# A state-space scan across five engines: tanh for the gate's Silu, and four instructions moved in the pipeline

## The chip, the cores and the metric

The kernel runs on one core of one Trainium2 chip. A core has TensorE (PE in the profile; its weight loads are shown as PEld), VectorE (DVE), ScalarE (ACT), GpSimd (POOL) and SyncE (SP, which here only issues DMAs). Each engine takes its instructions in the order of its own list; engines wait for one another through semaphores. The metric is the device time of one execution in microseconds (us).

## The reference

Two layers follow each other on an image batch of 4 x 48 x 48 x 128; each adds its result to its input. The change touches the first layer alone, a state-space scan over the image in four directions. Cut to what matters:

```python
xz = einsum(gn(x), in_proj_w); xin, z = split(xz)          # 256 channels each
xc = silu(depthwise_conv3x3(xin) + conv_b)
xs = [rows, columns, rows reversed, columns reversed] of xc  # K = 4 directions, L = 2304
dts_r, Bs, Cs = split(x_proj_w[k] @ xs[k])                   # 8, 16 and 16 rows
dt = softplus(dt_proj_w[k] @ dts_r + dt_proj_b)
for l in range(L):                                           # per channel, 16 states n
    h[n] = h[n] * exp(dt[l] * A[n]) + dt[l] * xs[l] * B[n, l]
    y[l] = sum(h[n] * C[n, l] for n in range(16))
y = sum of the four directions, turned back, + Ds * xs
out = out_proj_w @ (layernorm(y) * silu(z))
x = x + out
```

## The kernel before, in words

All work of the first layer is written out by hand in one order for every engine (`Ordered`, line 40, which is why the profile shows line 54 for nearly all of it). For each of 4 images the four directions run in the order k = 0, 2, 1, 3; each direction is cut into 5 chunks along the sequence, four of 480 places and one of 384. Within a chunk the 16 states are 16 steps. One step covers both halves of the 256 channels in one scan instruction of 2 x 480 + 2 places on VectorE.

Even and odd steps get their input dt * x * B in two ways:

- An even step: `spread` lets TensorE lay row B over all partitions in PSUM (`pb`, one bank); `drive_in` multiplies it with `du` on VectorE into `db`. Its decay exp(dt * A) is written by ScalarE into PSUM (`decay_here`, tile `da`, one buffer).
- An odd step: `scale` multiplies a transposed `du` (`turned`) with B as a per-partition factor on ScalarE (`scaled`, four instructions); `turn` transposes it back on TensorE into PSUM (a `da` bank, one buffer). Its decay is written by ScalarE to SBUF (`decay_there`, tiles `decay`, two buffers).

Then, for both, VectorE scans (`scan`, output `h`), GpSimd multiplies with row C (`read_out`, `hc`; the row `cbc` comes broadcast from DRAM by `fetch`, in ROWS = 5 buffers) and saves the carry; TensorE sums the `hc` of the states in PSUM by transposing into the same place (`sum_plain`, `sum_turned`, tiles `yp`, 16 instructions per pair of steps). After a chunk's last step `put_away` copies the sums to SBUF on ScalarE and lets a `gather` bring them back and add them to `y`.

`advance` (line 739) runs for each new step. It goes through the list `LAGS` (lines 733 to 736): a pair (3, fetch) means that `fetch` is issued for the step that came 3 steps ago. So the place in the list and the lag set the order in which each engine finds its instructions.

Everything else is cut into pieces by Python generators with `yield`: projecting the next direction's chunks (`project_chunk`: px, xd, pd, dt, bt), the next image's input projection and convolution (`front`: pj, pc, xc, pad), transposing `du` (`turn_du`: pdu), gathering (`gather`: pg, y or yb), and the end of an image's chunk (`back`: layer norm, gate, output projection; tile `ws`, matmuls pm, pv, pz, po, pr). `piece()` runs one piece, from one `yield` to the next; it is called at the end of each `advance`, and once more by `extra` for an odd step when more than one generator waits. Pieces use one PSUM bank in common (`side`, tag `pp`), so a piece's matmul waits until ScalarE or VectorE has read the one before.

The gate in `back` (lines 475 to 486): z = Silu(x W + b) from one instruction over both halves, after the norm's Ln and Exp; GpSimd multiplies it to `ys`. ScalarE holds one set of function tables at a time, and `ACT_TABLE_LOAD` changes it.

`done[0]` tells the projection of coming chunks which chunk has been used up, so that it may write to its `dt` and `bt` buffers again.

Of the kernel before, what the change touches and what calls it, by code (L numbers as in the profile page):

```python
# [12 lines left out]
AF = mybir.ActivationFunctionType  # L13
ALU = mybir.AluOpType
# [9 lines left out]
NF = D // 128  # L24
N = 16
# [6 lines left out]
LC = 480  # L32
GAP = 2
LB = 128
RING = 6
ROWS = 5
CHUNKS = [(s, min(LC, L - s)) for s in range(0, L, LC)]


# [18 lines left out]
def first_layer(ctx, tc, io, x1_dram, sp_dram, d_w, d_m):  # L58
# [9 lines left out]
    on = Ordered(tc)  # L68
# [9 lines left out]
    ps_y = ctx.enter_context(tc.tile_pool(name="l0_psy", bufs=1, space=PSUM))  # L78
    rows = ctx.enter_context(tc.tile_pool(name="l0_rows", bufs=ROWS))
    dram = ctx.enter_context(tc.tile_pool(name="l0_dram", bufs=8, space=DRAM))  # L80
# [60 lines left out]
    def side(name):  # L141
        pool, tag = banks[0]
        if not begun[0]:
            banks.rotate(-1)
        return pool.tile([128, 512], F32, tag=tag, name=name)
# [6 lines left out]
    def at(tile_, k, s, n):  # L152

        if k % 2 == 0:
            return tile_[:, :, s : s + n]
        return tile_.rearrange("p f (h w) -> p f w h", w=H)[:, :, s // T : (s + n) // T, :]

    def like(ap, k):

        return ap if k % 2 == 0 else ap.rearrange("p (w h) -> p w h", h=T)  # L160
# [6 lines left out]
    def open_up(b, x, made):  # L167

        xc = two.tile([128, NF, L], F32, tag="xc", name=f"xc{b}")
        made["xc"] = xc  # L170
        st = small.tile([128, 6, 6], F32, tag="st", name=f"st{b}", bufs=1)
        for q in range(6):
            on.vector.bn_stats(st[:, q], x[:, 0, q * 384 : (q + 1) * 384])
            if q % 2:
                yield FREE
        mv = small.tile([128, 2], F32, tag="mv", name=f"mv{b}")
        on.vector.bn_aggr(mv, st)
        aff = small.tile([128, 2], F32, tag="aff", name=f"aff{b}")
        group_affine(on, small, ps_s, gmat, eps, mv[:, 0:1], mv[:, 1:2], aff[:, 0:1], aff[:, 1:2], 1, f"g{b}")
        yield FREE  # L180
        wb = small.tile([128, 2 * NF], F32, tag="wb", name=f"wb{b}")
        pw = side(f"pw{b}")
        for q in range(2 * NF):
            on.tensor.matmul(
                pw[:, q : q + 1], w_in[:, q * 128 : (q + 1) * 128], aff[:, 1:2], start=True, stop=True
            )
        on.scalar.copy(wb, pw[:, 0 : 2 * NF])
        w = two.tile([128, 2 * D], F32, tag="w", name=f"w{b}")
        on.gpsimd.tensor_scalar(w, w_in, aff[:, 0:1], None, ALU.mult)
        made["w"], made["wb"] = w, wb  # L190
        yield FREE
# [163 lines left out]
    def blocks(n):  # L355

        return [(q, min(LB, n - q * LB)) for q in range(-(-n // LB))]
# [95 lines left out]
    def back(b, s, n, yb, x, w, wb):  # L453


        t = f"{b}_{s}"
        xs = at(x, 1, s, n)[:, 0]
        ys = yb[:, :, 0:n]
        ws = one.tile([128, (T + 2) * (H + 2)], F32, tag="pad", name=f"ws{t}")
        z = ws[:, 0 : NF * LC].rearrange("p (f n) -> p f n", f=NF)  # L460
        rs, xo = ws[:, NF * LC : (NF + 1) * LC], ws[:, (NF + 1) * LC : (NF + 2) * LC]
        pm = side(f"pm{t}")
        for f in range(NF):
            on.tensor.matmul(pm[:, 0:n], lnmat, yb[:, f, 0:n], start=(f == 0), stop=(f == NF - 1))
        yield
        on.vector.tensor_sub(ys, ys, pm[:, None, 0:n].to_broadcast([128, NF, n]))
        yield FREE
        on.scalar.activation(z[:, :, 0:n], ys, AF.Square)
        pv = side(f"pv{t}")
        for f in range(NF):  # L470
            on.tensor.matmul(pv[:, 0:n], lnmat, z[:, f, 0:n], start=(f == 0), stop=(f == NF - 1))
        yield

        on.scalar.activation(rs[:, 0:n], pv[:, 0:n], AF.Ln, bias=eps)
        for f in range(NF):
            pz = side(f"pz{t}_{f}")
            on.tensor.matmul(
                like(pz[:, 0:n], 1), w[:, D + f * 128 : D + (f + 1) * 128], xs, start=True, stop=True
            )
            yield  # L480
            if f == 0:
                on.scalar.activation(rs[:, 0:n], rs[:, 0:n], AF.Exp, scale=-0.5)
            on.scalar.activation(z[:, f, 0:n], pz[:, 0:n], AF.Identity, bias=wb[:, NF + f : NF + f + 1])
        on.scalar.activation(z[:, :, 0:n], z[:, :, 0:n], AF.Silu)
        yield FREE
        on.gpsimd.tensor_mul(ys, ys, z[:, :, 0:n])
        yield FREE
        po = side(f"po{t}")
        for f in range(NF):
            on.tensor.matmul(po[:, 0:n], w_out[:, 0, f], yb[:, f, 0:n], start=(f == 0), stop=(f == NF - 1))  # L490
        yield
        on.vector.tensor_mul(xo[:, 0:n], po[:, 0:n], rs[:, 0:n])
        pr = side(f"pr{t}")
        on.tensor.matmul(like(pr[:, 0:n], 1), ident, xs, start=True, stop=False)
        yield
        for f in range(NF):
            on.tensor.matmul(pr[:, 0:n], w_out[:, 1, f], z[:, f, 0:n], start=False, stop=(f == NF - 1))
        yield
        on.vector.tensor_add(xo[:, 0:n], xo[:, 0:n], pr[:, 0:n])
        last = b == B - 1 and s == 0  # L500
        (nc.scalar if last else nc.sync).dma_start(
            x1_dram[b].rearrange("w h t -> w (h t)")[:, s : s + n], xo[:, 0:n]
        )
        yield FREE
# [32 lines left out]
    def spread(u):  # L537

        c, i, n = u.c, u.i, u.c.n
        if i == N - 1:  # L540
            done[0] = c.number + 1
        if u.turned:
            return
        u.pb = ps_b.tile([128, 512], F32, tag="pb", name=f"pb{c.t}_{i}")
        for q, r in blocks(n):
            on.tensor.transpose(
                u.pb[:, q * LB : q * LB + r], c.bt[0:r, q, i : i + 1].to_broadcast([r, 128]), ident[0:r, 0:r]
            )
# [43 lines left out]
    def decay(u, turned):  # L592

        c, i, n = u.c, u.i, u.c.n
        if u.turned != turned:
            return
        da, o = (decays[i // 2 % 2], LC) if turned else (das[0], BANK - GAP)
        for f in range(NF):
            q = c.k * NF + f
            x = o + GAP if f else o - n  # L600
            on.scalar.activation(da[:, x : x + n], c.dt[:, f, 0:n], AF.Exp, scale=a_neg[:, q, i : i + 1])
        u.da = da[:, o - n : o + GAP + n]
# [48 lines left out]
    def gather(c, yt):  # L651
# [29 lines left out]
        if final:  # L681
            backs.append(back(c.b, s, n, yb, c.im["x"], c.im["w"], c.im["wb"]))
            later.append(backs[-1])
# [25 lines left out]
    done = [0]  # L709
# [17 lines left out]
    def drain(gen):  # L727
        while gen in later:
            piece()


    decay_here, decay_there = partial(decay, turned=False), partial(decay, turned=True)
    LAGS = (
        (3, fetch), (2, open_db), (4, drive_in), (5, scan), (4, decay_here), (3, spread), (4, turn), (3, decay_there),
        (2, extra), (2, scale), (5, read_out), (5, carry_on), (8, sum_plain), (7, sum_turned), (8, put_away),
    )
    window = deque([None] * 9, 9)

# [44 lines left out]
    for j, chunks in enumerate(directions):  # L783
# [9 lines left out]
        for m, c in enumerate(chunks):  # L793
            c.carry = carries[j % 2]
            for i in range(N):
# [7 lines left out]
                if m + 1 < len(chunks):  # L803
                    f = (6, 10).index(i) if i in (6, 10) else None
# [4 lines left out]
                elif nxt is not None:  # L809
                    f = (9, 12).index(i) if i in (9, 12) else None  # L810
# [19 lines left out]
def layer0(tc, io, x1_dram):  # L830

    io["first"] = partial(first_layer, tc, io, x1_dram)


def group_affine(nc, pool, psum, gmat, eps, mean, var, scale, shift, n, name):


    pm = psum.tile([128, 512], F32, tag="pp", name=f"gm_{name}")
    mc = pool.tile([128, n], F32, tag="gmc", name=f"gmc_{name}")
    nc.vector.tensor_copy(mc, mean)  # L840
    nc.tensor.matmul(pm[:, 0:n], gmat, mc, start=True, stop=True)
    gm = pool.tile([128, n], F32, tag="gm", name=f"gmean_{name}")
    nc.vector.tensor_copy(gm, pm[:, 0:n])
    d = pool.tile([128, n], F32, tag="gd", name=f"gd_{name}")
    nc.vector.tensor_sub(d, mc, gm)
    nc.vector.tensor_mul(d, d, d)
    nc.vector.tensor_add(d, d, var)
    pv = psum.tile([128, 512], F32, tag="pp", name=f"gv_{name}")
    nc.tensor.matmul(pv[:, 0:n], gmat, d, start=True, stop=True)
    sd = pool.tile([128, n], F32, tag="gs", name=f"gs_{name}")  # L850
    nc.scalar.activation(sd, pv[:, 0:n], AF.Sqrt, bias=eps)
    nc.vector.reciprocal(scale, sd)
    nc.vector.tensor_mul(shift, gm, scale)
    nc.vector.tensor_scalar_mul(shift, shift, -1.0)
# [1255 lines left out]
```

## Time and profile before

| | us |
|---|---|
| median of 3 runs (5062.57 to 5072.48) | 5067.83 |
| the profiled execution's own time | 5056.55 |
| its span | 5054.8 |
| PE busy | 4215.2 (83%) |
| DVE busy | 3822.8 (76%) |
| ACT busy | 3635.6 (72%) |
| POOL busy | 3367.5 (67%) |
| mean granted TensorE clock | 0.918 |

The first layer ends at about 4276 us of the span, where its last result is issued; the second layer takes the rest and is not changed. Busy times are sums over the whole span. "Idle before" is time that an engine spent without work just ahead of an instruction, and the name behind the arrow is what ended that wait. Starts in a timeline are in microseconds from the span's start.

### The profile page before, as it was taken

To read this page: it belongs to the slowest core of one execution; us is meant where nothing else is said; L and a number is where in the kernel's file an instruction comes from. 1 tells how busy PE (TensorE), PEld (TensorE's weight loads), DVE (VectorE), ACT (ScalarE), POOL (GpSimd) and SP (SyncE) were. 2 spreads that over 40 slices of the span, in tenths; PEclk is the share of its full clock that TensorE was granted. 3 is DMA by queue.
4 is the path that set the end of the run, shared out by engine and by line. 5 is a ranking of instruction groups with operands and counts; after the bars stand their busy time and mean duration, and the time that the engine had idled before them with its cause. 6 is when DMAs were issued, how large, how long until landed. Compare 5 with 4: busy or idle time off the path is not lost.

```text
span 5054.8 us, 73887 instructions
## 1 busy us (share of the span) xinstructions
PE 4215.2 (83%) x26332; PEld 3091.3 (61%) x26332; DVE 3822.8 (76%) x2574; ACT 3635.6 (72%) x7167; POOL 3367.5 (67%) x3533
## 2 busy tenths in 40 slices
PE   6888988887899888878998988787878786779976
PEld 3566766665666666656666666566666663445543
DVE  1587889877878898778788987788888985457636
ACT  3677788877777888787778887878888884413344
POOL 2476778766867787668676886677777874047631
PEclk8999999989999999899999998999999997889977
DMA  1122323222322232223232332223333323226546
GB/s 34 56 74 64 88 81 90 79 69 77 79 74 87 76 90 79 69 68 89 72 89 75 90 83 71 68 82 87 88 85 86 84 78 83 48 53 162 127 110 158
DMA packets 306204, 417.99 MB, mean 83 GB/s; under 512 B 110804, under 2 KB 285012, under 8 KB 305260
## 3 DMA queue, kind: packets, MB, share of 16 engines
q1 hardware_dynamic: 300256, 410.19, 30.5%
q8 instruction: 208, 3.41, 0.3%
q10 hardware_dynamic: 5580, 3.08, 0.2%
q14 instruction: 160, 1.31, 0.1%
HBM read 377.99 MB, written 35.38 MB: 82 GB/s over the span
## 4 chain that ended last, share of the span: by engine, by line
PE 47%; ACT 23%; DVE 12%; issue 7%; POOL 3%; DMA 2%; SPq 1%; DVEq 0%; ACTq 0%; POOLq 0%
PE yp L54 12%; DVE h L54 7%; PE da L54 6%; ACT scaled L54 5%; PE pg L54 5%; PE pc L54 4%; ACT da L54 4%; ACT decay L54 4%; PE pd L54 3%; PE px L54 3%; DVE db L54 3%; PE pb L54 2%; ACT dt L54 2%; ACT L54 2%; ACT ws L54 1%
## 5 line engine op out<-in xcount | busy, mean ns | idle before, releaser
L54 POOL TENSOR_TENSOR hc<-h,cbc 128x960 f32<-128x960 f32 (+1 forms) x1280 | 2540.2, 1985 | 1107.4 <-DVE h L54 665.1
L54 DVE TENSOR_TENSOR_SCAN h<-da,carry,db 128x962 f32<-128x962 f32 (+1 forms) x640 | 1359.6, 2124 | 369.5 <-ACT da L54 361.7
L54 DVE TENSOR_TENSOR_SCAN h<-decay,carry,da 128x962 f32<-128x962 f32 (+1 forms) x640 | 1365.5, 2134 | 25.5 <-PE da L54 18.5
L54 PEld LDWEIGHTS yp<-ident,hc 128*128 128x128 f32 (+1 forms) x9728 | 1180.3, 148 | 301.2 <-issue 166.4
L54 PE MATMUL yp<-ident,hc 128*128 128x128 f32 (+1 forms) x9728 | 1297.5, 289 | 63.9 <-ACT turned L54 28.7
L54 ACT ACTIVATE scaled<-turned,bt 128x256 f32<-128x256 f32 (+1 forms) x2432 | 1035.5, 497 | 3.7 <-PE da L54 3.7
L54 DVE TENSOR_TENSOR db<-du,pb 128x960 f32<-128x960 f32 (+1 forms) x640 | 704.8, 1101 | 408.5 <-PE pb L54 397.8
L54 ACT ACTIVATE da<-dt,a_neg 128x480 f32<-128x480 f32 (+1 forms) x1280 | 828.5, 647 | 175.3 <-DVE h L54 153.0
L54 ACT ACTIVATE decay<-dt,a_neg 128x480 f32<-128x480 f32 (+1 forms) x1280 | 791.4, 665 | 0.0
L54 PE MATMUL da<-ident,scaled 128*128 128x128 f32 (+1 forms) x4864 | 648.4, 277 | 107.5 <-DVE h L54 88.7
L54 PEld LDWEIGHTS da<-ident,scaled 128*128 128x128 f32 (+1 forms) x4864 | 553.4, 146 | 136.5 <-ACT decay L54 52.0
L54 PEld LDWEIGHTS pb<-ident,bt 128*128 128x128 f32 (+1 forms) x2432 | 295.1, 143 | 218.2 <-issue 173.4
L54 PE MATMUL pb<-ident,bt 128*128 128x128 f32 (+1 forms) x2432 | 381.9, 279 | 5.6 <-DVE db L54 5.4
L54 PE MATMUL pc<-pad,cdiag 128*128 128x480 f32 (+1 forms) x630 | 283.1, 574 | 8.8 <-ACT pad L54 8.8
L54 POOL TENSOR_TENSOR du<-dt,xc 128x480 f32<-128x480 f32 (+1 forms) x160 | 205.3, 1283 | 72.8 <-ACT dt L54 72.8
L1527 PE MATMUL acc<-v,attn_c 128*64 128x384 f32 x1152 | 207.6, 498 | 30.1 <-DVE v L1519 16.1
L1523 POOL TENSOR_TENSOR v<-grep,xrep 128x768 f32<-128x768 f32 x96 | 175.0, 1824 | 86.5 <-PE acc L1527 44.3
L54 ACT ACT_TABLE_LOAD x147 | 188.6, 1283 | 58.6 <-PE gv_l L54 35.1
L54 PE MATMUL px<-xc,w_xp 128*40 128x480 f32 (+1 forms) x320 | 214.0, 768 | 16.3 <-ACT xc L54 12.3
L1519 DVE TENSOR_TENSOR v<-gp,xrep 128x1536 f32<-128x1536 f32 x96 | 167.9, 1756 | 73.6 <-PE acc L1527 41.0
L54 PE MATMUL pdu<-ident,du 128*128 128x128 f32 (+1 forms) x608 | 110.9, 308 | 127.1 <-ACT turned L54 122.0
L54 PE MATMUL pg<-ident,turned 128*128 128x128 f32 x608 | 110.8, 303 | 124.4 <-ACT turned L54 93.2
(375 smaller groups left out, 4646.0 us busy)
## 6 DMA issues: line engine op xcount, KB each, us to landing
cbc<-cd SPq DMA_DIRECT2D x1024, 240.0 KB
cbc<-cd SPq DMA_DIRECT2D x256, 192.0 KB
xrep<-dxt SPq DMA_DIRECT2D x48, 576.0 KB
grep<-dgt SPq DMA_DIRECT2D x16, 576.0 KB
x<-in_xT SPq DMA_DIRECT2D x16, 288.0 KB
xr<-in_xT SPq DMA_DIRECT2D x16, 288.0 KB
da_m<-a_m SPq DMA_DIRECT2D x24, 192.0 KB
a_m<-da_m SPq DMA_DIRECT2D x32, 144.0 KB
```

What stands on the lines that cost most here:

```text
L54: return lambda *args, **kw: self._tc.keep_in_program_order(emit(*args, **kw))
L1519: nc.vector.tensor_mul(v, gp[:, None, :, 0:NC].to_broadcast([128, 2, 2, NC]), x[:, :, 0:2])
L1523: nc.gpsimd.tensor_mul(v3, r[:, 2:3].to_broadcast([128, 2, NC]), x[:, :, 2])
L1527: nc.tensor.matmul(acc[c][64 * b : 64 * b + 64, 0:NC], attn_c[:, 2 * pair + b, g, q], v[:, b, c] if c < 2 else v3[:, b], start=first, stop ...
```

## The change

Four things change together in the first layer.

1. The gate is computed as (tanh(a/2) + 1) * (a/2) with a = x W + b, which is Silu(a). The second half of the bias `wb` is stored halved; per half of the channels ScalarE writes a/2 into `z` and tanh(a/2) into a new view `th` of the same `ws` tile; then one VectorE instruction forms (th + 1) * z, ahead of GpSimd's multiplication.
2. `spread` moves from lag 3, ahead of `turn`, to lag 2 at the end of the list, behind the sums of the even step. One call of `piece()` lies between its old and its new place.
3. `decay_there` moves from lag 3 (behind `decay_here`) to lag 2, right behind `scale`; `extra` moves behind both. `put_away` moves from the end of the list to its beginning.
4. `fetch` moves from lag 3 to lag 1, and ROWS goes from 5 to 6.

`done[0]` is now set in `decay` for step N - 2, which is issued in the same `advance` as before.

```diff
-ROWS = 5
+ROWS = 6
...
-        on.scalar.copy(wb, pw[:, 0 : 2 * NF])
+        on.scalar.copy(wb[:, 0:NF], pw[:, 0:NF])
+        on.scalar.activation(wb[:, NF : 2 * NF], pw[:, NF : 2 * NF], AF.Copy, scale=0.5)
...
         z = ws[:, 0 : NF * LC].rearrange("p (f n) -> p f n", f=NF)
+        th = ws[:, 3 * LC : 5 * LC].rearrange("p (f n) -> p f n", f=NF)
...
-            on.scalar.activation(z[:, f, 0:n], pz[:, 0:n], AF.Identity, bias=wb[:, NF + f : NF + f + 1])
-        on.scalar.activation(z[:, :, 0:n], z[:, :, 0:n], AF.Silu)
+            bias = wb[:, NF + f : NF + f + 1]
+            on.scalar.activation(z[:, f, 0:n], pz[:, 0:n], AF.Identity, bias=bias, scale=0.5)
+            on.scalar.activation(th[:, f, 0:n], pz[:, 0:n], AF.Tanh, bias=bias, scale=0.5)
         yield FREE
+        on.vector.scalar_tensor_tensor(z[:, :, 0:n], th[:, :, 0:n], 1.0, z[:, :, 0:n], ALU.add, ALU.mult)
         on.gpsimd.tensor_mul(ys, ys, z[:, :, 0:n])
...
     def spread(u):
-        if i == N - 1:
-            done[0] = c.number + 1
         if u.turned:
             return
...
     def decay(u, turned):
         if u.turned != turned:
             return
+        if i == N - 2:
+            done[0] = c.number + 1
...
     LAGS = (
-        (3, fetch), (2, open_db), (4, drive_in), (5, scan), (4, decay_here), (3, spread), (4, turn), (3, decay_there),
-        (2, extra), (2, scale), (5, read_out), (5, carry_on), (8, sum_plain), (7, sum_turned), (8, put_away),
+        (1, fetch), (8, put_away), (2, open_db), (4, drive_in), (5, scan), (4, decay_here), (4, turn),
+        (2, scale), (2, decay_there), (5, read_out), (5, carry_on), (2, extra), (8, sum_plain), (7, sum_turned),
+        (2, spread),
     )
```

## The prediction

> **What bounds the kernel now.** I read the busy shares first: no engine is over 83%, so a chain through several engines decides. Then the windows: the first layer, where the whole change lies, takes about 4276 of 5055 us. Then the costliest groups of the page; the columns behind the bar are busy us, mean ns of one, and the engine's idle time just before them with its releaser.
>
> ```profile
> L54 DVE TENSOR_TENSOR_SCAN h<-da,carry,db 128x962 f32<-128x962 f32 (+1 forms) x640 | 1359.6, 2124 | 369.5 <-ACT da L54 361.7
> L54 DVE TENSOR_TENSOR_SCAN h<-decay,carry,da 128x962 f32<-128x962 f32 (+1 forms) x640 | 1365.5, 2134 | 25.5 <-PE da L54 18.5
> ...
> L54 DVE TENSOR_TENSOR db<-du,pb 128x960 f32<-128x960 f32 (+1 forms) x640 | 704.8, 1101 | 408.5 <-PE pb L54 397.8
> ...
> L54 ACT ACT_TABLE_LOAD x147 | 188.6, 1283 | 58.6 <-PE gv_l L54 35.1
> ```
>
> A pair of steps (even e, odd e+1) is one `drive_in` and two scans on DVE: 1359.6 + 1365.5 + 704.8 = 3430 us over 640 pairs. What is not that work is mostly two waits: the `drive_in` waits 398 us for the spread B (`pb`, PE), the even scan 362 us for its decay (`da`, ACT). The odd scan almost never waits. Undisturbed, a pair takes 5.3 us on DVE (`drive_in` at 1566.93 and at 1572.24 in DVE's timeline). The wait for `pb` must be read from a place where it happens; PE's timeline, then DVE's (start, length, instruction, idle before it):
>
> ```profile
> 1576.48 1.78 PE L54 MATMUL pc<-pad,cdiag 128*128 128x480 f32 x4
> 1578.09 0.57 PE L54 MATMUL pb<-ident,bt 128*128 128x128 f32 x4
> 1578.51 0.99 PE L54 MATMUL da<-ident,scaled 128*128 128x128 f32 x8
> ```
>
> ```profile
> 1578.71 1.16 DVE L54 TENSOR_TENSOR db<-du,pb 128x960 f32<-128x960 f32 x1 [1.06 <-PE pb L54]
> 1579.78 2.22 DVE L54 TENSOR_TENSOR_SCAN h<-decay,carry,da 128x962 f32<-128x962 f32 x1
> ```
>
> PE runs without a gap here: a piece (a convolution's matmuls), the spread, the turn for the odd scan. The `drive_in` is late by 1.06 us, and the odd scan 1.07 us after it starts just when the turn is done (about 1579.6). The turn alone would have held it to the same time.
>
> The second place is the gate, in a chunk of the image's last direction (k=3); ACT, PE, DVE:
>
> ```profile
> 1044.65 1.28 ACT L54 ACT_TABLE_LOAD   x1
> 1045.94 1.01 ACT L54 ACTIVATE ws<-ws 128x960 f32<-128x960 f32 x1
> 1046.85 1.69 ACT L54 ACTIVATE scaled<-turned,bt 128x256 f32<-128x256 f32 x4
> 1048.56 1.28 ACT L54 ACT_TABLE_LOAD   x1
> 1049.85 1.36 ACT L54 ACTIVATE da<-dt,a_neg 128x480 f32<-128x480 f32 x2
> ```
>
> ```profile
> 1052.94 1.11 PE L54 MATMUL pdu<-ident,du 128*128 128x128 f32 x4 [5.37 <-ACT turned L54]
> ...
> 1056.58 3.13 PE L54 MATMUL yp<-ident,hc 128*128 128x128 f32 x16
> ```
>
> ```profile
> 1051.30 2.22 DVE L54 TENSOR_TENSOR_SCAN h<-da,carry,db 128x962 f32<-128x962 f32 x1 [3.63 <-ACT da L54]
> ```
>
> Two loads and the Silu stand between two even decays, so the scan waits 3.63 us. PE idles 5.37 us behind ACT, and its next sums take 3.13 us where an undisturbed PE took 1.91 (1045.65): the clock is lower after a long gap, not after one of 0.84 (1587.68).
>
> **The change, part by part.**
>
> *Spread earlier.* It passes one piece on PE, not the turn. Where PE is the late one, as at 1578, everything ahead of the turn still stands ahead of it, so the 1.06 us leave the `drive_in` and come back before the odd scan. Worth 0 to -0.1 us a time. Only where PE is late for the spread but has idle time before the turn is there a gain. The spread now waits for the `drive_in` two steps before; that stands ahead of a scan which the preceding turn feeds, and 16 sums (1.9 us) lie between, so this wait is hidden. Of 398 us I expect 300 to move to the odd scan.
>
> *Odd decay (ACT) with the scaling.* Same instructions, 2 x 0.66 us. On ACT the stretch between two even decays holds the same work as before, so the even scan's date changes only through waits. The new one: the decay's buffer is freed by the odd scan of four steps before, which ends 3.2 us after the start of the last even decay, while ACT arrives after 1.3 + 1.6 = 2.9 us. Queued behind it on ACT are evictions and the next even decay, which cannot start before 5.3 us anyway. Cost 0; if the even decay is already late, up to 0.3 us a pair.
>
> *Extra piece behind the scaling and odd decay.* ACT does 2.8 us of free work before an eviction of PE's results instead of after it, good for ACT (it waits 165 us for `pc`, 125 for `pd`). But the eviction comes some 1.6 us later for PE, which has one bank for pieces and waits for it. Bounds for both together: one such wait per chunk removed or added, 80 x 0.7 us, so +-56. I take 0, as the nearest rows (PE `pdu` waiting 122 us, `pg` 93 for ACT) do not show which is late.
>
> *put_away earlier.* The copies of finished sums (1.1 us) pass the scaling and the drain of earlier gathers. They can now wait for the sums, at most 1 us; what queues behind is scaling, with slack. The gather's transposes start earlier, but its first eviction now stands before the even decay, a wait for PE. In a k=1 chunk the 1.52 us wait of the `drive_in` at step 6 (1824.93) turns into about 1.1 before the even scan and 0.8 before the `drive_in`: +0.2 us. In k=3 the waits of 0.70, 1.12 and 3.51 at steps 2 and 6 become one of 3.7 for the mean's matmul: -1.8.
>
> *Rows two steps ahead, a sixth buffer.* 1280 SP issues move past everything SP issues within two steps. SP waits for POOL's release either way (3568 us in SP's waits); POOL waited 22.8 us in all for these rows. Bounds -22.8, and +22.8 if as much again is added by stores of `cd` that queue behind a blocked issue; I take 0, as SP's waits are for POOL, which works at the same pace.
>
> *Gate.* 39 loads fewer in the program's order, x 1.283 = -50 us; Silus of 1.01 (16) and 0.83 (4) (the square of that width) go, -19.5; 40 tanhs of half a tile come, the price bounded by 0.56 and 0.66 (activations of the same shape out of PSUM), 0.63 taken: +25. ACT -44. DVE gets 20 (tanh+1)*z of 960: bounded by 0.65 (480 wide) and 2.2 (the scan), I take the add-like row of this shape, 1.13: +22, in DVE's own queue behind ACT's tanh.
>
> The Trainium skill, "ScalarE: Activation LUTs", "What ACT_TABLE_LOAD costs", counts 2.66 us for each switch, a drain included; by it the loads alone would be worth an estimated 104 us. Here the next activation starts 0.01 us after the load's 1.28 (1045.94), so the trace decides.
>
> *A middle chunk of k=3 walked through in the new order*, from scan 0's end at 1011.97 (next such point before: 1074.1), each engine's list taken in order, each operation at its own length in this chunk; worked-out times. ACT: copies end 1015.5, scaling 1017.1, odd decay 1018.3, first eviction 1019.05, even decay (4) 1020.35. PE: second gather 1021.3, sums 1023.05, spread 1023.45, turn 1024.6, mean 1026.3; DVE subtracts to 1027.35 and ends scan 6 at 1032.7 (before 1034.5: -1.8). ACT: square 1028.35, scaling, odd decay (waits for scan 5) 1031.7, load, Ln, load, Exp 1035.5, half gate and tanh 1036.75, even decay (8) 1038.05, so scan 8 waits 2.15. PE waits for each of these, runs slow, and ends spread 10 at 1042.4, turn 9 at 1043.5, the piece behind it 1044.1; even decay (10) 1045.95, scan 10 ends 1048.1 (before 1053.5: -5.4). Now the gate's end stands back to back: DVE's new operation to 1049.2, POOL's 2.22 us product to 1052.6, `po` on PE after a gap of 4 us, so slow, to 1055.4, sums 1058.4, spread, `pr`, turn, `pr` 1063.5. DVE's two closing operations, now before scan 12 and before step 14's `drive_in`, wait 3.0 and 5.4 us for them, where they waited 0.18 and 0.85. Scan 14 ends 1069.4 (before 1068.8): +0.6 us for the chunk.
>
> On that clock the Trainium skill speaks against the change: "TensorE: Matmul & The Clock Gate", "HAM oscillation", warns of gaps over some 3.4 us. The trace shows the drop already after 2.12 us (sums of 3.02 at 1022.60), and the walk goes by that. By the page the gaps of 1.3 and 1.95 us around the gate's matmuls would leave PE fast, sums 1.5 us shorter in 20 chunks, an estimated 30 us less.
>
> *Sum.* Middle k=3 chunks of images 0 to 2: 6 x +0.6 = +4. Their last chunks, where the gather's wait (3.56) halves and the gate's three waits (2.25, 1.94, 1.53) lose the loads: 3 x -4 = -12. The back that runs into the next image (5.12 before step 10): 3 x -2.5 = -8. Image 3's four gates and the one at the end: -11. The k=0 chunk that opens the next image (3.87 + 1.90 + 2.82), whose copies no longer stand behind the first step of that work: 3 x -2.5 = -8. Other chunks 0. Together -35 us. The profiled execution took 5056.6 (span 5054.8), 11 below the median of 5067.8; 5021.6 on its scale, 5033 on the median's.
>
> **The rivals.**
>
> A. Forecast: waits move, the gate pays: -11 to -80.
>
> B. The early spread pays in full. For it: 398 us, the largest wait of DVE. Against: at 1578 the turn is due at the same time. If half went: -200, 4870.
>
> C. Slower, by DVE's two waits at the gate's end (walked at 8.4 us). From 1.75 us more in each of 20 chunks they eat the 35; at half as much again, +4.2 x 20 - 35 = +49, 5117; at twice, +133. For it: PE's gap and slow clock right before, and DVE's strict order, so that the scans wait with them. Against: ACT, which made PE late there (5.37 us), has 44 us less to do.
>
> D. No change beyond what a measurement can tell, 0.2% or 10 us: waits merely renamed. For it: same PE work, the same ACT work between decays.
>
> **How the numbers follow.** A 0.47, B (100 us and more) 0.15, C 0.26, D 0.12. So faster 0.62, same 0.12, slower 0.26. The range cuts a tenth at each end: below, B's lesser half (-140: 4928); above, C to +45 or 5113. A's own range is 4988 to 5057.
>
> **What would show it.** The wait of `db` for `pb` falls well under 150 us, and the odd scan's for PE `da` rises from 18.5 to 200 or more; if it stays under 60, B is right. Loads 108 or so. k=3 middle chunks of 60 to 65 us, with new waits of `ws` for `po` and `pr` (19 and 16 us in all before) of over 80 together; if these exceed 170, C. I am wrong if pieces meet the decays otherwise than walked through, which shows in the wait for ACT `da` (362 now, 330 expected).

## The result, and the profile after

The changed kernel takes 5159.65 us (median of 4 runs, 5155.77 to 5163.5) against 5070.15 (4 runs, 5062.57 to 5074.53) for the kernel before: 1.0178 times as long, 95% interval 1.016 to 1.0196. A gain of 35 us had been forecast, with a range that ended at 5113. The profiled execution took 5155.77 us (before: 5056.55), so its trace shows 99 us more, at a mean granted clock of 0.903 (0.918).

The page's groups of the changed kernel, those shown of before (busy us, mean ns of one | idle just before them and its releaser):

```profile
L54 DVE TENSOR_TENSOR_SCAN h<-da,carry,db 128x962 f32<-128x962 f32 (+1 forms) x640 | 1359.8, 2125 | 379.1 <-ACT da L54 370.4
L54 DVE TENSOR_TENSOR_SCAN h<-decay,carry,da 128x962 f32<-128x962 f32 (+1 forms) x640 | 1365.0, 2133 | 153.6 <-PE da L54 144.5
...
L54 DVE TENSOR_TENSOR db<-du,pb 128x960 f32<-128x960 f32 (+1 forms) x640 | 701.9, 1097 | 207.8 <-PE pb L54 201.4
```

The `drive_in`'s wait fell from 398 to 201 us and the odd scan's rose from 18.5 to 144.5: that much of the early spread is a wait with a new name. The even scan's wait for its decay, which should have fallen to 330, is 370. The loads, in the list of groups, then waits of the changed kernel (us in all, times, longest):

```profile
L54 ACT ACT_TABLE_LOAD x108 | 138.6, 1283 | 58.4 <-PE gv_l L54 36.4 <-PE gv_g L54 13.4 <-issue 7.0
```

```profile
PE po L54 <- POOL yb L54: 85.4, 20, 5.1
...
DVE ws L54 <- PE po L54: 80.7, 20, 6.0
...
DVE ws L54 <- PE pr L54: 66.7, 18, 4.8
```

39 loads are gone, 50 us of ScalarE. But VectorE's two closing operations of `back` now wait 147 us for `po` and `pr`; before it was 37.3 and 20.5, of which 18.2 and 4.7 belong to the very last back, after all scans (6.0 and 4.8 in the changed kernel). Beside scans it is 137 us against 35. Added up from the first scan of the first layer to its last, VectorE idles 80 us more: 187 less ahead of the `drive_in`, but 126 more ahead of the odd scan, 102 for `po` and `pr`, 28 for the mean's matmul `pm` (0 before) and 9 ahead of the even scan. In all 20 chunks that have a `back`, PE itself waits for the gate's product by POOL. One such place, in a middle chunk of k=3, in the timelines of PE, DVE and POOL (start, length, instruction, idle before it):

```profile
2128.06 0.31 PE L54 MATMUL da<-carry,ident 128*128 128x2 f32 x2
2133.41 3.57 PE L54 MATMUL po<-yb,w_out 128*128 128x480 f32 x4 [5.04 <-POOL yb L54]
2136.77 2.39 PE L54 MATMUL yp<-ident,hc 128*128 128x128 f32 x16
```

```profile
2128.02 1.13 DVE L54 SCALAR_TENSOR_TENSOR ws<-ws 128x960 f32<-128x960 f32 x1
2129.07 1.15 DVE L54 TENSOR_TENSOR db<-du,pb 128x960 f32<-128x960 f32 x1
2130.13 2.21 DVE L54 TENSOR_TENSOR_SCAN h<-decay,carry,da 128x962 f32<-128x962 f32 x1
2137.02 0.66 DVE L54 TENSOR_TENSOR ws<-po,ws 128x480 f32<-128x480 f32 x1 [4.67 <-PE po L54]
```

```profile
2128.24 2.82 POOL L54 TENSOR_TENSOR hc<-h,cbc 128x960 f32<-128x960 f32 x1 [0.21 <-PE da L54]
2131.01 0.17 POOL L54 COPY carry<-h 128x2 f32<-128x2 f32 x1
2131.16 2.20 POOL L54 TENSOR_TENSOR yb<-yb,ws 128x960 f32<-128x960 f32 x1
```

This is the chain that the walk had: gate on DVE, product on POOL, `po` after a gap and slow, and DVE held. Ahead of the gate's product (`yb`) POOL has another one to do, the `read_out` of a step (`hc`). PE has nothing to do for 5.04 us, because the sums that follow at 2136.77 stand behind `po` in its list. No scan starts for 4.67 us, because the next one stands behind DVE's closing operation.

Of the 99 us, 93.5 lie between the first and the last scan of the first layer. What stands ahead of the first scan and behind the last is 8 us shorter, and the second layer, which the change leaves alone, 14 us longer; over all the profiled runs it takes 779 to 795 us, whatever is changed. Where the 93.5 came from, by VectorE's chunk periods (from the first scan of a chunk to that of the next, changed kernel less before; chunks of a direction are numbered from 0):

| | forecast, us | measured, us |
|---|---|---|
| k=3, chunks 2 and 3, images 0 to 2 (walked) | +4 | +18.7 |
| k=3, last chunk, images 0 to 2 | -12 | +1.8 |
| k=0, chunk 0, images 1 to 3 (the back that runs over) | -8 | +12.4 |
| k=0, chunk 2, images 1 to 3 | -8 | -2.3 |
| k=3, image 3 (the forecast counts the last back too, which behind the scans took 2.1 less) | -11 | -3.4 |
| all other chunks | 0 | +66.4 |

The last row is +20.1 in image 0's k=0, +10.3 in the rest of k=0, +13.3 in k=2, +12.6 in k=1 and +10.1 in the first two chunks of k=3. So there is more than one place.

### The profile page after: what moved, and what is told of

It is laid out like the page before. It is cut to its first block, busy times and chain, and to the rows that moved or that the text cites. A ratio compares the mean times of both kernels' runs of the same rounds, so it can differ in the third digit from the quotient of the medians.

```text
span 5154.0 us, 73742 instructions
## 1 busy us (share of the span) xinstructions
PE 4283.3 (83%) x26332; PEld 3121.2 (61%) x26332; DVE 3838.8 (74%) x2594; ACT 3618.7 (70%) x7152; POOL 3375.9 (66%) x3533
## 4 chain that ended last, share of the span: by engine, by line
PE 50%; ACT 19%; DVE 13%; issue 6%; POOL 3%; DMA 2%; SPq 1%; DVEq 0%; POOLq 0%; ACTq 0%
PE yp L54 13%; DVE h L54 8%; PE da L54 6%; PE pc L54 4%; PE pg L54 4%; ACT scaled L54 4%; PE px L54 3%; PE pd L54 3%; ACT decay L54 3%; PE pb L54 2%; DVE db L54 2%; ACT da L54 2%; ACT dt L54 2%; ACT turned L54 2%; PE acc L1532 2%
## 5 line engine op out<-in xcount | busy, mean ns | idle before, releaser
L54 DVE TENSOR_TENSOR_SCAN h<-decay,carry,da 128x962 f32<-128x962 f32 (+1 forms) x640 | 1365.0, 2133 | 153.6 <-PE da L54 144.5
L54 PEld LDWEIGHTS yp<-ident,hc 128*128 128x128 f32 (+1 forms) x9728 | 1211.8, 151 | 261.3 <-issue 157.5
L54 PE MATMUL yp<-ident,hc 128*128 128x128 f32 (+1 forms) x9728 | 1329.1, 293 | 18.9 <-POOL hc L54 16.5
L54 ACT ACTIVATE decay<-dt,a_neg 128x480 f32<-128x480 f32 (+1 forms) x1280 | 796.2, 671 | 124.7 <-DVE h L54 120.1
L54 PEld LDWEIGHTS pg<-ident,turned 128*128 128x128 f32 x608 | 78.3, 163 | 222.7 <-ACT y L54 124.4
L54 PE MATMUL pd<-xd,w_dt 40*128 40x480 f32 (+1 forms) x320 | 171.7, 618 | 38.2 <-ACT xd L54 26.2
```

Of the source, the lines that this page charges most:

```text
L54: return lambda *args, **kw: self._tc.keep_in_program_order(emit(*args, **kw))
```

## The experiments

All variants compute the whole result. Times are medians; the ratio, with its 95% interval, is to the kernel before on the same chip.

**One part alone, on the kernel before.** The gate (its lines as in the diff above):

> The kernel before with the tanh gate alone, its pipeline order untouched. If the walk was right that the gate pays where it does not meet the new order (two loads fewer per back on ACT, one VectorE operation more), it is faster by 20 to 50 us, the wait of the even scan for ACT da falls from 362 by 30 or more, and the waits of ws for po and pr stay under 60 us together (35 before). If the gate itself brings the loss (the VectorE operation queued behind ACT's tanh and ahead of the scans), it is slower by 30 us or more and those waits are near the changed kernel's 147 us.

The spread:

```diff
-(4, decay_here), (3, spread), (4, turn), ... (8, put_away),
+(4, decay_here), (4, turn), ... (8, put_away), (2, spread),
```

> The kernel before with spread alone moved to lag 2 behind the sums. If the wait is only renamed, the time stays within 10 us, the wait of db for pb falls from 398 to about 200, and the odd scan's wait for PE da rises from 18.5 to about 150 to 200 us. If the early spread pays, it is faster by 50 us or more. If a piece ahead of the turn costs more than a piece ahead of the spread, it is slower by 20 to 50 us.

The odd decay and `extra` behind the scaling; for `extra` this is also behind `read_out` and `carry_on`:

```diff
-(4, turn), (3, decay_there), (2, extra), (2, scale), (5, read_out), (5, carry_on), (8, sum_plain),
+(4, turn), (2, scale), (2, decay_there), (5, read_out), (5, carry_on), (2, extra), (8, sum_plain),
```

> The kernel before with decay_there at lag 2 behind scale, and extra behind both; spread, put_away, fetch and gate as before. If the loss of the changed kernel comes from pieces that now stand back to back with nothing of ACT between them, it is slower by 50 to 100 us and most of the waits of PE for ACT are longer. If these moves are neutral, as predicted, it is within 15 us.

`put_away` at the head:

```diff
-(3, fetch), (2, open_db), ... (7, sum_turned), (8, put_away),
+(3, fetch), (8, put_away), (2, open_db), ... (7, sum_turned),
```

> The kernel before with put_away alone moved to the head of the list. If the gather's first eviction ahead of the even decay costs as in the walk of a k=1 chunk, those chunks (44 us) change by 0 to +2 us, and the time by -20 to +20 us. If the copies waiting for the sums hold up the scaling, it is slower by 40 us or more, and ACT's wait of turned for yp rises from some 12 us to over 60.

The rows:

```diff
-ROWS = 5 ... (3, fetch)
+ROWS = 6 ... (1, fetch)
```

> The kernel before with fetch at lag 1 and ROWS 6 alone. If SP only waits earlier for POOL (theory), within 10 us. The four other parts alone gave +0, +18, -18 and -27 us, the whole change +90; if the rows bring the missing 117 us, this one is slower by 60 us or more, and POOL's wait for DMA cbc (22.8 us before) or ACT's wait of xd for its store is far longer.

**Taken back from the changed kernel.** The spread at its old place:

> The changed kernel with spread back at lag 3 ahead of turn. If an early spread does its harm only together with the other moves (a piece's matmul between it and the turn, on which the extra piece, its eviction and then the even decay now wait), this wins back most of the 90 us: faster than the changed kernel by 60 to 110. If the parts interact elsewhere, it wins back about 18, as the spread cost alone.

`extra` and the odd decay at their old places:

> The changed kernel with extra and decay_there back in their old places. If the two pieces standing back to back at the odd step's end are the cause together with the early spread or early put_away, this wins back 50 to 110 us of 90. If the extra's move is good in every company, as it was alone, this is slower than the changed kernel by about 18 us.

And two parts together, on the kernel before: `extra` and the odd decay behind the scaling, and `put_away` first.

> The kernel before with both moves that were faster alone: extra and decay_there behind scale, put_away at the head. If the gains add, faster than before by 45 us, about 5025. If these two are what does not go together (the gather's pieces then fall on extra and on the end of the same step, so that its first eviction stands ahead of the even decay), slower than before by 20 us or more, above all in k=3.

| | us | ratio [95%] |
|---|---|---|
| gate alone | 5071.34 | 0.9998 [0.9984, 1.0011] |
| spread alone | 5088.81 | 1.0045 [1.0027, 1.0064] |
| extra and odd decay alone | 5052.39 | 0.9966 [0.9953, 0.9979] |
| put_away alone | 5043.33 | 0.9939 [0.9917, 0.996] |
| rows alone | 5069.81 | 0.9996 [0.9986, 1.0005] |
| changed, spread back | 5144.82 | 1.0144 [1.0129, 1.0159] |
| changed, extra and odd decay back | 5115.48 | 1.0082 [1.0066, 1.0099] |
| extra, odd decay and put_away | 5155.28 | 1.0172 [1.0151, 1.0193] |

Added up, the single parts give -26 us against a kernel before of 5070.4: close to the forecast's -35, which added parts in the same way. Two of them, each a gain by itself (-18 and -27), together cost 85, nearly the whole loss. Yet taking one of these two, `extra` with the odd decay, back out of the changed kernel wins back only 44 us: the losses of the parts overlap. The spread, rival B's gain, costs 18 alone and 15 within the change.

What the pair does shows in the orders of the lists. With `put_away` first, a gather is put in the queue of pieces before the `extra` of the same step instead of after it, so it and all that queues behind it (the back above all) run one slot earlier. There are three slots per pair of steps: the piece of the even step, `extra`, and the piece of the odd step. The last two are neighbours: PE's 16 sums do not stand between them. In a middle k=3 chunk the pieces that need each other's results (the halves of the norm's matmul `pz`, the transposes `pdu`, `po` after the gate) then meet on the neighbours, where before PE had the 16 sums between them.

That alone is not the loss. By their traces, PE and VectorE go through the same order of work with `put_away` alone, which gains 27 us, as with the pair. `extra`'s move changes only two other lists. On ScalarE its piece now comes behind the scaling. On GpSimd it comes behind `read_out` and `carry_on`: a gate's product that falls on `extra` has one product more ahead of it, while `po` stands on PE right behind the turn and waits. Alone, `extra`'s move does this only where a gate's product falls on `extra` in the kernel before, in the last k=3 chunk of images 0 to 2. There it costs 7.2 us each time; the middle chunks gain 3.6 to 5.5.

**A slot later.** If it is the neighbours together with these orders, one empty slot cures it without touching any of the moved instructions:

```diff
 def gather(c, yt):
     ...
+    yield FREE
     for f in range(NF):
```

The changed kernel with it, then the pair with it:

> The changed kernel, with one empty yield at the head of gather, so that the pieces of a gather (and all that queue behind them) come one slot later, as they did with put_away at the end of the list. Theory of the slots (put_away first puts two dependent pieces on the neighbouring slots of one odd step, with nothing between them on PE or ACT once extra stands behind the scaling): most of the 90 us come back, 5070 to 5100; k=3 middle chunks near 62, the first chunk of k=0 near 61, the waits of ws for po and pr under 80 together (147 in the changed kernel), po for POOL under 50. Rival, that the order of ACT's instructions within a step costs the time wherever the pieces fall: 5145 to 5170, waits as in the changed kernel. Rival, that put_away's copies themselves at the head of the list cost it: also 5145 to 5170.

> The kernel before with extra and the odd decay behind the scaling, put_away first (those two together gave 5155), and an empty yield at the head of gather. Theory of the slots: the order on PE in k=3 is again that of the kernel before, so 5030 to 5065, between the two parts alone (5052 and 5043). Rivals (order within the step, or the early copies): 5145 to 5165.

The odd decay's share, and the gate beside put_away (on the kernel before, `put_away` first in both):

> The kernel before with put_away first and the odd decay right behind the scaling, but extra left ahead of the scaling. Theory of the slots: extra's evictions stay early on ACT, with the scaling between them and the next piece, so it stays near put_away alone, 5035 to 5065. Rival, that the moved odd decay makes the loss together with put_away: 5110 to 5160. If it lies between, 5070 to 5105, both have a share.

> The kernel before with put_away first and the gate by tanh. If the parts add up (put_away alone -27, the gate alone +1): 5040 to 5050. If the gate is freed by put_away's earlier pieces, as the prediction's walk through a k=3 chunk had it (44 us of ACT less): 5000 to 5030. If the gate's shorter work on ACT brings two dependent pieces nearer, as extra behind the scaling does: 5080 or more, with waits of ws for po and pr of 120 or more together.

And the controls: the empty slot alone; with put_away first; two empty slots with the pair; one with the pair and the gate:

> The kernel before with one empty yield at the head of gather and nothing else. If it is the slot (three per pair of steps, the kernel before's being a good one): slower, 5085 to 5150, the loss in k=3. If a later gather is better by itself: 4990 to 5045. If a slot more or less means nothing here: within 10 us of the kernel before.

> put_away first and one empty yield at the head of gather: the pieces are on the kernel before's slots, and only the copies of the sums (and the wait on them) stand at the head of the list. If the copies' earlier place is a gain of its own (extra, decay and put_away with this yield gave 5006, extra and decay alone 5052): 5010 to 5035. If the gain needs extra's place: 5055 to 5075.

> Extra and the odd decay behind the scaling, put_away first, and two empty yields at the head of gather. With none it took 5155, with one 5006. If it is the slot, the second yield moves the pieces to the third place of the pair, and some of the 149 us go again: 5060 or more. If a later gather is better in any case: 4990 to 5015, as with one.

> Extra and the odd decay behind the scaling, put_away first, one empty yield, and the gate by tanh. If the gate's loads (39 of 1.28 us) are on the path once the slots are right: 4960 to 4990. If the gate stays neutral, as alone: 4995 to 5015. If its shorter work on ACT again brings dependent pieces nearer: 5030 to 5060.

| | us | ratio [95%] |
|---|---|---|
| changed kernel, one empty slot | 5027.09 | 0.9922 [0.9903, 0.9941] |
| extra, odd decay and put_away, one empty slot | 5005.91 | 0.9879 [0.9861, 0.9897] |
| odd decay and put_away | 5115.58 | 1.0091 [1.0073, 1.011] |
| gate and put_away | 5082.21 | 1.002 [1.0007, 1.0032] |
| one empty slot alone | 5069.03 | 0.9999 [0.999, 1.0009] |
| put_away, one empty slot | 5018.05 | 0.9902 [0.9887, 0.9916] |
| extra, odd decay and put_away, two empty slots | 5113.77 | 1.0089 [1.0072, 1.0106] |
| extra, odd decay, put_away and gate, one empty slot | 4995.39 | 0.9859 [0.9842, 0.9876] |

One empty slot takes 133 us off the changed kernel and 149 off the pair, more than expected, and a second one gives 108 of these 149 back. So neither the copies at the head nor the order within a step makes the loss by itself, and a later gather isn't better in any case: it is where the pieces fall in that order. A lower mean clock is not what makes the changed kernel slow: with the empty slot it has 0.902 in its profile and takes 5025 us. What a good slot looks like, in a middle k=3 chunk of the pair with one empty slot (PE and DVE):

```profile
2067.16 1.94 PE L54 MATMUL yp<-ident,hc 128*128 128x128 f32 x16
2070.03 1.88 PE L54 MATMUL po<-yb,w_out 128*128 128x480 f32 x4 [0.93 <-POOL yb L54]
2071.74 0.57 PE L54 MATMUL pb<-ident,bt 128*128 128x128 f32 x4
```

```profile
2069.89 2.20 DVE L54 TENSOR_TENSOR_SCAN h<-da,carry,db 128x962 f32<-128x962 f32 x1
2072.01 0.63 DVE L54 TENSOR_TENSOR ws<-po,ws 128x480 f32<-128x480 f32 x1
```

and the same place with no empty slot:

```profile
2135.71 3.57 PE L54 MATMUL po<-yb,w_out 128*128 128x480 f32 x4 [4.27 <-POOL yb L54]
2139.07 2.59 PE L54 MATMUL yp<-ident,hc 128*128 128x128 f32 x16
```

```profile
2139.32 0.66 DVE L54 TENSOR_TENSOR ws<-po,ws 128x480 f32<-128x480 f32 x1 [4.97 <-PE po L54]
2139.89 2.21 DVE L54 TENSOR_TENSOR_SCAN h<-da,carry,db 128x962 f32<-128x962 f32 x1
```

In the good slot PE does the sums (1.94 us) while POOL multiplies, waits 0.93 and takes 1.88 for `po`, not 3.57; DVE has an even scan between the product and the closing operation and waits for nothing. In the bad one the sums stand behind `po`. The chunk takes 55.2 us against 65.2.

Three expectations fell. The empty slot alone was to lose in k=3 and is neutral: a middle chunk does lose (64.0 for 62.2 us, with 5.99 us of waiting for `po`), but the last chunk of k=3 gains (62.2 for 65.6), k=2 loses up to 9 us per direction, and image 3 gains 22 in all. So a slot is good or bad for the pieces that meet there; no rule for all chunks came out. The gate beside put_away lost 39 us against put_away alone, though not by waits of 120 for `po` and `pr` (54.7 and 54.8). And the odd decay beside put_away took 5116 where the slots gave 5035 to 5065. That called for two more:

> put_away first, the odd decay right behind the scaling (extra ahead of it), and one empty yield at the head of gather; without the yield 5116, against 5018 with the yield and without the odd decay's move. If the odd decay harms through the slots of the pieces: 5005 to 5035. If its place on ScalarE harms by itself beside early copies: 5080 to 5120.

> put_away first and extra behind the scaling, the odd decay left at lag 3. If the two moves add on put_away's 5043 (the odd decay +72, both +112): 5070 to 5100. If either move is enough to make most of the loss: 5110 to 5150. If extra harms only with the odd decay: 5035 to 5060.

The first took 5134.09 (1.0126 [1.0109, 1.0143]), still above what was expected, the second 5124.29 (1.0111 [1.0092, 1.013]). These are two mechanisms, each told by its own wait (of the wait for `po`, 18.3 and 17.4 us are the last back). Put_away first with `extra` behind the scaling, the odd decay left where it was:

```profile
DVE h L54 <- ACT da L54: 344.6, 161, 21.6
...
DVE ws L54 <- PE po L54: 90.1, 20, 18.3
PE po L54 <- POOL yb L54: 87.5, 20, 5.7
```

Put_away first, one empty slot, and the odd decay behind the scaling with `extra` ahead of both:

```profile
DVE h L54 <- ACT da L54: 471.8, 247, 21.6
...
DVE ws L54 <- PE po L54: 17.4, 1, 17.4
PE po L54 <- POOL yb L54: 14.5, 10, 5.4
```

`extra`'s move makes the wait for `po` (37.5 with put_away alone) and doesn't touch the even scan's (344.0 there). How, the same middle k=3 chunk of image 1 shows, POOL and PE, with put_away alone:

```profile
2065.59 2.22 POOL L54 TENSOR_TENSOR yb<-yb,ws 128x960 f32<-128x960 f32 x1
2067.76 2.07 POOL L54 TENSOR_TENSOR hc<-h,cbc 128x960 f32<-128x960 f32 x1
...
2067.86 1.88 PE L54 MATMUL po<-yb,w_out 128*128 128x480 f32 x4 [1.89 <-POOL yb L54]
```

and with `extra` behind the scaling too:

```profile
2104.89 2.05 POOL L54 TENSOR_TENSOR hc<-h,cbc 128x960 f32<-128x960 f32 x1 [1.62 <-issue]
...
2107.03 2.21 POOL L54 TENSOR_TENSOR yb<-yb,ws 128x960 f32<-128x960 f32 x1
...
2109.29 3.57 PE L54 MATMUL po<-yb,w_out 128*128 128x480 f32 x4 [5.68 <-POOL yb L54]
```

The two products on POOL have changed places. The gate's is 3.8 us later (POOL idles 1.62 us ahead of the `read_out`, which takes 2.05), so PE waits 5.68 us instead of 1.89 and `po` takes 3.57 instead of 1.88. Until then this chunk was 1.5 us ahead of the other; it ends 4.5 us longer. Counted over the trace, the gate's product has one more product ahead of it in exactly 12 chunks, the last four of k=3 in images 0 to 2. These 12 make 62 of the 82 us that the first layer's scans take longer. So the main step is GpSimd's order, not ScalarE's.

The odd decay's move, without `extra`'s, leaves `po` alone and makes the even scan wait 149 us more than the same kernel without it (322.6 with put_away and one empty slot, 5018 us), and 84 more without the empty slot (427.5 against 344.0). Here PE, VectorE and GpSimd keep their orders, so it is ScalarE's. That list offers a reason: with `extra` ahead of the scaling, the odd decay's 1.28 us no longer stand ahead of the evictions of two pieces, and come between the second and the next even decay. One place, a middle chunk of k=1, shows the second half of this (ScalarE, then VectorE), with put_away and one empty slot:

```profile
1809.10 1.35 ACT L54 ACTIVATE da<-dt,a_neg 128x480 f32<-128x480 f32 x2
...
1810.54 2.22 DVE L54 TENSOR_TENSOR_SCAN h<-da,carry,db 128x962 f32<-128x962 f32 x1
```

and with the odd decay moved as well:

```profile
1853.82 1.27 ACT L54 ACTIVATE decay<-dt,a_neg 128x480 f32<-128x480 f32 x2
1855.00 1.34 ACT L54 ACTIVATE da<-dt,a_neg 128x480 f32<-128x480 f32 x2
...
1856.43 2.22 DVE L54 TENSOR_TENSOR_SCAN h<-da,carry,db 128x962 f32<-128x962 f32 x1 [1.31 <-ACT da L54]
```

In both, ScalarE has waited 2.34 us for the piece's eviction, and the scaling follows; the even decay begins 2.39 us after the eviction's start in the first and 3.58 in the second. With `extra` moved as well (5006 us) the free work stands ahead of the eviction again. No run separates this reason from others. One of them is ScalarE's new wait for the odd decay's buffer, which the odd scan frees: none with the odd decay at its old place, 102.1 us with it moved and no empty slot, 60.1 with the slot. It cannot be enough, since the kernel of 5006 us has 73.9 us of it and an even scan that waits 335. Nor was the odd decay moved alone without put_away.

Best of all is the last of the table, the pair with one empty slot and the gate, without the early spread and the early rows: 4995.39 us, 3.2% below the changed kernel and 1.41% below the one before. The gate's share of that is not clear of the noise (0.9859 [0.9842, 0.9876] against 0.9879 [0.9861, 0.9897] without it).

## Why the prediction was wrong

- **Extra piece behind the scaling and odd decay.** The step that failed. The text took 0 between ±56, as the nearest rows "do not show which is late". Alone (with the odd decay) it is -18, inside the bounds, but beside an early put_away it is +112 (5155 against 5043), outside them: the bound of one wait of 0.7 us per chunk came from waits for an eviction. The text priced what `extra` passes on ScalarE and PE; that it also passes `read_out` on GpSimd, and so puts one more product of 2.05 us ahead of the gate's, is nowhere in the sum. Beside an early put_away, without the odd decay, that move is +81 (5124 against 5043), with waits of 4 to 5 us for `po` in the last four k=3 chunks of an image, where put_away alone has none. The walk's times leave room for that product, but it was never set against an order that does without.
- **Odd decay with the scaling** at 0 was wrong by itself too: beside put_away, with `extra` left ahead, it costs 72 us (5116 against 5043) and with the empty slot 116 (5134 against 5018). The text looked at when the decay's buffer comes free, which it priced at up to 0.3 us a pair (ScalarE waits 120.1 us for it in the changed kernel, 0.19 a pair), not at the free work that the odd decay's old place gave ScalarE ahead of an eviction.
- **put_away earlier** was given some microseconds in k=1 and k=3. Alone it is -27, more than forecast, and -51 with the old slots kept. Its other effect, that the gather and everything behind it move by one of three slots, was in the walk of one chunk, but not carried to the others.
- **The sum.** Each part was priced against the kernel before and the prices were added. Measured alone, the parts do add up to nearly the forecast (-26); the loss is in parts that meet: 85 for put_away with `extra` and the odd decay, and 39 more for put_away with the gate than for put_away alone.
- **The walk of a middle k=3 chunk** was right in kind and near in size: waits for `po` and `pr` of 3.0 and 5.4 walked, 4.67 and 4.13 measured, for `pm` 3.7 and 3.69, for the even scan at step 8 2.15 and 2.51. The chunk came out at +3.1 instead of +0.6. But it was compared only with the kernel before: that these 8 us were new, 20 times, and that an order without them was one slot away, was not asked. The chunks called "others, 0" brought +66.
- **Last k=3 chunks and the back that runs over** were to gain 20 from the loads; they lost 14. Their closing waits grew as in the middle chunks (4.56 and 4.52 us in the last chunk of image 1, 0 and 3.15 before).
- **Gate.** Loads 147 to 108, as said, and the even scan's wait falls by 51 us (362.0 to 310.6). But the time of the gate alone doesn't change: the wait for `po`, in all 20 chunks now, rises from 19 to 41 us beside scans, and the pieces meet other work (-3.3 us in k=3, +9.4 in k=2, per direction). With good slots it is worth some 10 us, if anything (the intervals overlap), not 44. The Trainium skill's "What ACT_TABLE_LOAD costs" ("ScalarE: Activation LUTs") would have made the loads alone an estimated 104; no run here shows more than these 10.
- **Spread earlier.** Right in kind: 196 us left the `drive_in`, 126 came back at the odd scan. But "0 to -0.1 a time" had the wrong sign: 15 to 20 us are lost. With the spread moved alone, 230 us leave the `drive_in` between the first scan and the last; 134 come back at the odd scan under PE's name, 68 there under ScalarE's, and 24 at the even scan's decay. Which piece makes the loss was not tested.
- **Rows** at 0: right.
- **Rival C** had the mechanism and the place; at its half-as-much-again price it gave 5117. Its own mark, over 170 us of waits for `po` and `pr`, was not reached (147), and the kernel is yet slower than that: waits elsewhere, such as the even scan's 370 for a forecast 330, came on top. **Rival B** is excluded by the odd scan's 144.5.

## What to carry to other kernels

Where pieces of work are dealt into fixed slots, moving an instruction past the dealer moves every piece after it; ask first which pairs of dependent pieces then fall next to each other, and what independent work stood between them. Moving the dealer puts every instruction that it passes ahead of the piece, on each engine: go through the lists of all of them, the idle ones too. Prices of parts measured or argued one at a time do not add in such a pipeline. When a reordering loses, try shifting its phase by one empty slot before taking it back: here that one line turned +1.8% into -0.8%.

## What the runs showed of the hardware

In the changed kernel, 19 of the 20 new gate operations on VectorE, which read two tiles in SBUF, run beside one of POOL's products, and each of these products takes 2.62 to 2.89 us. All the other 1005 products of that shape, and all 1024 in the kernel before, take at most 2.09 (mean 2.06). At 2128.24 above this is 0.76 us on the chain to `po`, which the walk did not have (POOL's clock of events is rough, but the difference repeats). The Trainium skill says as much: in "SBUF — State Buffer", "Who interferes with whom", a VectorE instruction with two inputs in SBUF contends with a GpSimd instruction that reads SBUF.

PE after a gap: `po` took 3.57 us behind 4.27 and 5.04 us of idle time, 1.88 behind 0.93. In between the gap's length alone doesn't tell: behind 2.79 us it took 1.88 in the kernel before (at 2275.53) and 3.57 with the empty slot alone (at 2100.49).
